# Root on VectorE, category rows by products, and more rows by address in a recommender kernel

## The chip, the core and the metric

The kernel runs on one core of a Trainium2 chip. The metric is device time in microseconds of one execution. Engines are named as in the profile: PE (TensorE), DVE (VectorE), ACT (ScalarE), POOL (GpSimd) and SP (SyncE). SP, ACT and POOL also issue DMAs; in the profile their issuing shows as SPq, ACTq and POOL.

## The reference

There are B = 16384 candidates, each with a user, an item, a category and a history of L = 200 items. Embeddings have 64 numbers.

```python
u = u_emb[user]; it = i_emb[item]; c = c_emb[cate]; h = i_emb[hist]     # h: (200, B, 64)
itb = jnp.broadcast_to(it[None], h.shape)
feat = jnp.concatenate([h, itb, h - itb, h * itb], axis=-1)
a = dice(feat @ au_W1 + au_b1, au_alpha, axis=1)    # mean and variance over B, per layer
w = a @ au_W2 + au_b2
cur = jnp.sum(w * h, axis=0)
z = jnp.concatenate([u, it, c, cur], axis=-1)
z = dice(z @ W1 + b1, alpha1, axis=0)
z = dice(z @ W2 + b2, alpha2, axis=0)
return z @ W3 + b3
```

dice(x) is x * (p + alpha * (1 - p)) with p = sigmoid((x - mean) / sqrt(var + 1e-8)). The item and user tables have 100,000 rows of 256 bytes, the category table has 1,000. All numbers are 32-bit floats. The work is dominated by 200 x 16384 rows of the item table.

## The kernel before

One history position l is a layer. A layer is cut into ND = 8 steps, and a step k = 8 l + c handles TD = 16 tiles of 128 rows (2048 candidates). A `rows` buffer holds the 16 tiles of a step, and there are 5 of these buffers.

Rows reach a buffer in two ways. Most tiles come by a gather: POOL issues one indirect DMA (L123) for 128 rows, with the row numbers from the tile `idx`. The last tile of some steps comes row by row: for the steps c in SIDES = (1, 3, 4, 5, 6, 7), SP and ACT load row addresses into registers (L293, up to 20 at a time) and issue one DMA of 256 bytes per row (L301) into one of 3 `side` buffers; ACT waits for all 128 rows on a semaphore (`await_rows`, L309) and copies the tile into its place in `rows` (`place`, L352). Step c = 5 does so only where l % 3 == 0 (SOMETIMES, EACH); otherwise its last tile is gathered with row numbers from `sidx`. So a layer with l % 3 == 0 has six tiles by address, and 122 gathers; the others have five, and 123 gathers. The rows by address of a layer are spread over its 8 steps, half of each step's on SP, half on ACT: 48 or 40 rows per step and queue.

The order is written out by hand; every engine runs its queue in that order. In step k: the gathers of step k; on ACT the hidden layer of step k - 2 (`hidden`, L339); at the end of a layer the statistics and the normalization (`moments`, `scale_and_shift`, L170 to L172, with the square root on ACT, which needs a table load before it and one after it, for the sigmoid); on ACT the sigmoid of step k - 9 (`gate`, L328); the wait and copy of the row tile of step k - 1; the row DMAs of step k; on DVE the transposes of step k - 1 (`turn`, L156), which also free the `rows` buffer for POOL; on PE and DVE the products of step k - 1; on DVE the statistics (L344), then `weights` (L331) and `weigh` (L335, L336) of step k - 9.

SP carries, besides its rows, the loads for the next layer: `idx` (L136) in step 0, `sidx` (L142) where needed, and the addresses (L145) in step 2.

In the prologue the items of all candidates are gathered (128 gathers) and transposed into `itT`, and the weights are loaded. The loop body covers 45 layers and runs 4 times, and 20 layers follow. In the tail, users and categories are gathered (256 gathers), a user step and a category step by turns, and the head is computed: the first layer with its statistics as the tiles come, then the rest.

Of the kernel before, what the change touches and what calls it, by code (L numbers as in the profile page):

```python
# [27 lines left out]
EACH = 3  # L28
LOAD = 20
ROW = 4 * D  # L30
# [4 lines left out]
def din_kernel(  # L35
# [76 lines left out]
    ids = [make(f"ids{i}", P, NT, dt=I32) for i in range(3)]  # L112
# [17 lines left out]
    def load_ids(t, v):  # L130
        nc.sync.dma_start(t[:, :NC], columns(v))
        for s in range(NS):
            nc.sync.dma_start(t[:, NC + s : NC + s + 1], col(v[(NC + s) * P : (NC + s + 1) * P]))

# [9 lines left out]
    def load_addresses(i, l):  # L144
        nc.sync.dma_start(addr[i], r_hist[ds(l, 1), NC * P :])  # L145
# [21 lines left out]
    def scale_and_shift(mean, var, rstd, shift):  # L167
        n = mean.shape[0]
        std = small.tile([P, 1], F32, tag="std", name="std")
        nc.scalar.activation(std[:n], var, AF.Sqrt, bias=eps[:n])  # L170
        nc.vector.reciprocal(rstd, std[:n])
        nc.vector.scalar_tensor_tensor(shift, mean, -1.0, rstd, ALU.mult, ALU.mult)  # L172

    eps = make("eps", P, 1)
# [14 lines left out]
    def attention_weights():  # L189
        nc.vector.memset(eps, EPS)  # L190
# [45 lines left out]
    def head_weights():  # L236
# [3 lines left out]
        for e in range(2):  # L240
            for g in range(2):
                r, d = quarter(e, g), ts(e, S)
                nc.sync.dma_start(w1a[r, :, ts(g, ZA)], w1[d, :, :ZA])
                nc.sync.dma_start(w1b[r, :, ts(g, ZB)], w1[d, :, ZA:])
        for g in range(2):
            nc.sync.dma_start(w2a[ts(g, ZA), g * ZA : g * ZA + Z2], W2[:ZA])
# [20 lines left out]
    flat = i_emb.rearrange("v d -> (v d)").bitcast(U8)  # L267

# [4 lines left out]
    def tiles_by_address(l):  # L273

        round_, i = divmod(l, EACH)
        first = round_ * (EACH * (NS - 1) + 1) + i * (NS - 1) + (i > 0)
        return first, [j for j, c in enumerate(SIDES) if has_side(l * ND + c)]

    def rows_by_address(k):
        l, s = divmod(k, ND)  # L280
        first, tiles = tiles_by_address(l)
        n = len(tiles) * P // ND // 2
        loads = -(-n // LOAD)
        for i, (engine, issue) in enumerate(
            ((mybir.EngineType.SP, nc.sync), (mybir.EngineType.Activation, nc.scalar))
        ):
            r0, end = (2 * s + i) * n, (2 * s + i + 1) * n
            while r0 < end:
                many = min(end - r0, -(-n // loads))
                at0 = tiles[r0 // P] * P + r0 % P  # L290
                while tiles[(r0 + many - 1) // P] * P + (r0 + many - 1) % P != at0 + many - 1:
                    many -= 1
                _, at = nc.values_load_multi_w_load_instructions(  # L293
                    addr[l % 3][:, at0 : at0 + many],
                    engines=(engine,), min_val=0, max_val=ROW * (V - 1),
                    skip_runtime_bounds_check_because="the DMA checks the address against the table",
                )
                for r, a in enumerate(at, r0):
# [9 lines left out]

    def await_rows(m):  # L309
        if m in keys:  # L310
            fence = nc.scalar.wait_ge(landed[m % 3], 16 * P)
            tc.declare_fence(fence.ins, group=keys.pop(m))
            nc.scalar.sem_clear(landed[m % 3])

    def has_side(k):
        l, c = divmod(k, ND)
        return c in SIDES and (c != SOMETIMES or l % EACH == 0)
# [28 lines left out]
    def place(k):  # L346
        if has_side(k):
            l, c = divmod(k, ND)
            first, tiles = tiles_by_address(l)
            m = first + tiles.index(SIDES.index(c))  # L350
            await_rows(m)
            nc.scalar.copy(rows[k % ROWS][:, TD - 1], side[m % 3])  # L352
# [30 lines left out]
    def step(k, last=None):  # L383
# [12 lines left out]
        if has(k - LAG):  # L396
            gate(k - LAG)
        if has(k - 1):
            place(k - 1)
        if has(k):  # L400
            rows_by_address(k)
        if has(k - 1):
# [5 lines left out]
        if has(k - LAG):  # L408
# [3 lines left out]
    def steps(l0, n, end):  # L412
        for k in range(n * ND):
            l, c = divmod(k, ND)
            if c == 0 and l + 1 < end:
                load_hist_ids((l + 1) % IDX, l0 + l + 1)
                if (l + 1) % EACH:
                    load_side_ids((l + 1) % IDX, l0 + l + 1)
            if c == 2 and l + 1 < end:
                load_addresses((l + 1) % 3, l0 + l + 1)  # L420
            if c == 4 and l + 1 < end:
                scale_addresses((l + 1) % 3)
            step(k)

    with tc.manual_schedule():
        load_ids(ids[0], r_item)
        load_hist_ids(0, 0)
        load_addresses(0, 0)
        load_ids(ids[1], r_cate)
        load_ids(ids[2], r_user)  # L430
        nc.gpsimd.iota(lanes, pattern=[[1, P]], base=P, channel_multiplier=-1)
        attention_weights()
        for t in (*hT, *xs, *side, hm):
            nc.vector.memset(t, 0.0)
        for t in curT:
# [7 lines left out]
        scale_addresses(0)  # L443
        layer(px, [(blk_m, hm)])

        for c in range(ND + 1):
            if c < ND:
                for n in range(TD):
                    j = column(c, n)
                    gather(rows[c % ROWS], ids[0][:, j : j + 1], n, i_emb)  # L450
            if c:
                transpose(itT[c - 1], rows[(c - 1) % ROWS])
        nc.vector.memset(rows[-1 % ROWS], 0.0)
# [17 lines left out]
    def head_fetch(k, j):  # L471
        c, u = divmod(j, 2)
        for n in range(TD):
            i = column(c, n)
            gather(rows[k % ROWS], ids[1 + u][:, i : i + 1], n, (c_emb, u_emb)[u])

    def head_layer(j):
        c, u = divmod(j, 2)
        if u == 0:
            pairs = ((2, ucT[j % 4]), (1, itT[c]), (3, curT[c]))  # L480
        else:
            pairs = ((0, ucT[j % 4]),)
# [118 lines left out]
```

## Time and profile before

| what | value |
|---|---|
| median of 10 runs | 51,004.96 us (50,974.05 to 51,075.69) |
| profiled execution: its time, its span | 50,960.83 us, 50,959.1 us |
| busy: PE, DVE, ACT, POOL | 41%, 30%, 9%, 46% of the span |
| row DMAs issued by SP, by ACT | 68,288 each |
| gathers on POOL | 24,533 of history, 128 of items, 128 of users, 128 of categories |
| mean granted TensorE clock | 0.694 |

Busy shares are of work in the engines; register instructions, semaphores and the issuing of DMAs by SP and ACT do not count as busy. In the lines of groups, the columns are: line, engine, operation, output and inputs, count, then busy time in all and nanoseconds of one, then idle time before them with what ended it. In a timeline, they are start, duration, engine, line, operation, tile and count, and in square brackets the idle time before.

### The profile page before, as it was taken

The page shows a single profiled execution, that of the slowest core. Times are in us where ns is not written, and L with a number is a line of the kernel's source. Part 1 is how long each engine was busy: PE and PEld are TensorE (multiplying, and loading weights), DVE is VectorE, ACT ScalarE, POOL GpSimd, SP SyncE. Part 2 cuts the span into 40 slices and gives each one's busy share as a digit, 9 for nine tenths or more (in the row PEclk, how much of TensorE's full clock was granted, in tenths as well). Part 3 has the DMA queues.
Part 4 walks back from the last instruction along what each step waited for, and adds up shares of the span by engine and source line. Part 5 has one row for each costly group of instructions (what it writes and reads, how often), then busy time and mean ns, then how long its engine had stood idle before and what let it go on. Part 6 is the DMA issues. An engine that isn't in the chain of part 4 may idle for free. (4 is left out here: it accounts for less than half of the span.)

```text
span 50959.1 us, 423966 instructions
## 1 busy us (share of the span) xinstructions
PE 20882.2 (41%) x38856; PEld 8541.7 (17%) x38856; DVE 15096.3 (30%) x18955; ACT 4416.1 (9%) x4941; POOL 23571.8 (46%) x24922
## 2 busy tenths in 40 slices
PE   3444444443444444444444444434444444444444
PEld 1111111111111111111111111111111111111111
DVE  2322232232222222222222222222223222222223
ACT  0000000000000000000000000000000000000001
POOL 5444444444444444444444444444444444444444
PEclk6666667676676666666676666666676666666667
DMA  1000100000000000000010001000000000100000
GB/s 19 18 17 17 18 17 18 17 17 18 18 18 17 17 18 17 17 18 17 17 18 17 17 18 18 17 17 18 17 18 18 18 17 18 18 17 18 18 17 17
DMA packets 1130924, 894.71 MB, mean 18 GB/s; under 512 B 729024, under 2 KB 729024, under 8 KB 1127896
## 3 DMA queue, kind: packets, MB, share of 16 engines
q0 software_dynamic: 797344, 818.07, 9.1%
q1 hardware_dynamic: 193112, 31.56, 0.4%
q10 hardware_dynamic: 137440, 17.76, 0.2%
q14 instruction: 2722, 22.30, 0.1%
q8 instruction: 306, 5.01, 0.0%
HBM read 865.10 MB, written 0.13 MB: 17 GB/s over the span
## 5 line engine op out<-in xcount | busy, mean ns | idle before, releaser
L123 POOL DMA_INDIRECT rows<-in_L_rec_i_emb,idx x24400 | 23082.3, 946 | 26994.0 <-DVE hT L156 19317.1
L161 PE MATMUL ph<-hT,unit 128*128 128x512 f32 x6404 | 5968.8, 1087 | 28850.7 <-DVE hT L156 27817.0
L335 DVE SCALAR_TENSOR_TENSOR wb<-wb,au_bias,hT 128x1024 f32<-128x1024 f32 x1609 | 2080.0, 1293 | 20967.4 <-remote 16592.7
L156 DVE STREAM_TRANSPOSE hT<-rows 64x512 f32<-64x512 f32 x6404 | 4516.2, 705 | 9866.5 <-ACT rows L352 9715.8
L161 PEld LDWEIGHTS ph<-hT,unit 128*128 128x128 f32 x6404 | 1798.6, 311 | 31910.2 <-DVE hT L156 30520.0
L339 ACT ACTIVATE xs<-px,au_bias 128x1024 f32<-128x1024 f32 x1602 | 1785.0, 1114 | 45005.6 <-issue 40412.7
L161 PE MATMUL px<-hT,blk_h 128*128 128x512 f32 x6404 | 4070.6, 723 | 979.2 <-ACT xs L339 623.6
L161 PE MATMUL px<-itT,blk_i 128*128 128x512 f32 x6404 | 3466.5, 624 | 0.0
L161 PE MATMUL wb<-y,blk_p 128*128 128x512 f32 x6436 | 3296.2, 594 | 46.8 <-issue 26.4
L161 PE MATMUL wb<-xs,blk_x 128*128 128x512 f32 x6436 | 3295.8, 594 | 27.0 <-DVE curT L336 16.8
L161 PE MATMUL px<-hm,blk_m 128*128 128x512 f32 x6408 | 3013.0, 592 | 69.5 <-remote 69.5
L344 DVE BATCH_NORM_STATS2 st<-xs 128x6 f32<-128x512 f32 x3204 | 2061.3, 685 | 2896.4 <-ACT xs L339 2232.0
L360 DVE TENSOR_TENSOR hm<-ph,itT 128x1024 f32<-128x1024 f32 x1601 | 1956.9, 1222 | 1659.8 <-PE ph L161 1285.1
L161 PEld LDWEIGHTS px<-hT,blk_h 128*128 128x128 f32 x6404 | 1609.1, 254 | 3531.9 <-issue 2700.5
L336 DVE TENSOR_TENSOR curT<-wb,curT 128x1024 f32<-128x1024 f32 x1609 | 1970.2, 1225 | 54.8
L331 DVE TENSOR_TENSOR y<-pg,xs 128x1024 f32<-128x1024 f32 x1609 | 1954.9, 1215 | 21.6 <-issue 21.4
L328 ACT ACTIVATE pg<-xs,sh,rs 128x1024 f32<-128x1024 f32 x1609 | 1934.1, 1202 | 30.8 <-DVE y L331 16.4
L161 PEld LDWEIGHTS px<-itT,blk_i 128*128 128x128 f32 x6404 | 1404.7, 219 | 1987.5 <-issue 1987.5
L161 PEld LDWEIGHTS wb<-y,blk_p 128*128 128x128 f32 x6436 | 1225.2, 190 | 1594.1 <-issue 1568.4
L161 PEld LDWEIGHTS wb<-xs,blk_x 128*128 128x128 f32 x6436 | 1224.5, 190 | 1573.8 <-issue 1553.3
L161 PEld LDWEIGHTS px<-hm,blk_m 128*128 128x128 f32 x6408 | 1218.0, 190 | 1604.5 <-issue 1534.3
L352 ACT COPY rows<-side 128x64 f32<-128x64 f32 x1068 | 251.2, 235 | 591.2 <-DMA side<-in_L_rec_i_emb 495.7
(155 smaller groups left out, 2148.3 us busy)
## 6 DMA issues: line engine op xcount, KB each, us to landing
side<-in_L_rec_i_emb SPq DMA_DIRECT2D x68288, 0.2 KB
side<-in_L_rec_i_emb ACTq DMA_DIRECT2D x68288, 0.2 KB
rows<-in_L_rec_i_emb,idx POOLq DMA_INDIRECT x24400
idx<-in_r_hist SPq DMA_DIRECT2D x200, 61.0 KB
addrs<-in_r_hist SPq DMA_DIRECT2D x200, 3.0 KB
sidx<-in_r_hist SPq DMA_DIRECT2D x133, 0.5 KB
rows<-in_L_rec_i_emb,sidx POOLq DMA_INDIRECT x133
rows<-in_L_rec_i_emb,ids POOLq DMA_INDIRECT x128
```

The costliest lines, as they stand in the source:

```text
L123: nc.gpsimd.indirect_dma_start(out=dst[:, n, :], out_offset=None, in_=table, in_offset=bass.IndirectOffsetOnAxis(ap=ids, axis=0),)
L156: nc.vector.transpose(by_tile(dst[ts(e, D)], i), of[ts(i, D), :, ts(e, S)])
L161: nc.tensor.matmul(dst[:, ts(i, CH)], lhsT, rhs[:, ts(i, CH)], start=(first and j == 0), stop=(last and j == len(pairs) - 1), skip_group_c ...
L328: nc.scalar.activation(pg, xs[k % XR], AF.Sigmoid, bias=shifts[i], scale=rstds[i])
L331: nc.vector.tensor_mul(y, pg, xs[k % XR])
L335: nc.vector.scalar_tensor_tensor(wb, wb, au_bias2, hT[k % LAG], ALU.add, ALU.mult)
L336: nc.vector.tensor_add(curT[k % ND], wb, curT[k % ND])
L339: nc.scalar.activation(xs[k % XR], px, AF.Identity, bias=au_bias)
L344: nc.vector.bn_stats(stats[l % 3][:, 2 * c + i, :], xs[k % XR][:, ts(i, CH)])
L352: nc.scalar.copy(rows[k % ROWS][:, TD - 1], side[m % 3])
L360: nc.vector.tensor_mul(hm, ph, itT[k % ND])
```

## The change

1. The square root and its reciprocal move from ACT to DVE: a first guess from the bits of the number by a shift and an integer-like multiply-add, then three Newton steps of three operations.
2. The wait for a row tile, the clearing of its semaphore and the copy into `rows` move from ACT to DVE.
3. Step c = 5 has its tile by address where l % 3 is 0 or 1 (MOST = 2): two layers of three have six tiles by address. In a step, all of SP's row DMAs and the first load's worth of ACT's stand ahead of the gate, the rest of ACT's after it.
4. In the prologue, the last tile of six of the eight item steps comes by address, 0.56 of the rows on SP. Meanwhile the category rows are made by products: the category numbers are laid out in order in memory, spread over 125 partitions, compared with 8 columns of values (`pick_categories`), and PE multiplies the table with the ones and zeros. The result, transposed as it is needed, is stored in memory (`catT`). Several zeroings go from DVE to ACT as copies of zeros.
5. In the tail there are 8 steps in place of 16: users are gathered, 5 of their tiles by address; the categories are loaded from `catT`; two steps of `gate`, `weights` and `weigh` are done per step while any are left. The weight rows of the category features are laid out for the new order.

```diff
--- before.py
+++ after.py
@@ -26,7 +26,9 @@
 SIDES = (1, 3, 4, 5, 6, 7)
 SOMETIMES = 5
 EACH = 3
+MOST = 2
 LOAD = 20
+SPLIT = 0.5
 ROW = 4 * D
...
-    ids = [make(f"ids{i}", P, NT, dt=I32) for i in range(3)]
+    ids = [make(f"ids{i}", P, NC, dt=I32) for i in range(2)]
...
     def scale_and_shift(mean, var, rstd, shift):
         n = mean.shape[0]
-        std = small.tile([P, 1], F32, tag="std", name="std")
-        nc.scalar.activation(std[:n], var, AF.Sqrt, bias=eps[:n])
-        nc.vector.reciprocal(rstd, std[:n])
+
+        v = small.tile([P, 1], F32, tag="v", name="v")
+        h = small.tile([P, 1], F32, tag="h", name="h")
+        v, h = v[:n], h[:n]
+        nc.vector.tensor_scalar_add(v, var, EPS)
+        nc.vector.tensor_single_scalar(h.bitcast(I32), v.bitcast(I32), 1, ALU.logical_shift_right)
+        nc.vector.tensor_scalar(
+            rstd.bitcast(I32), h.bitcast(I32), -1.0, float(0x5F375A00), ALU.mult, ALU.add
+        )
+        for _ in range(3):
+            nc.vector.scalar_tensor_tensor(h, rstd, v, rstd, ALU.mult, ALU.mult)
+            nc.vector.tensor_scalar(h, h, -0.5, 1.5, ALU.mult, ALU.add)
+            nc.vector.tensor_mul(rstd, rstd, h)
         nc.vector.scalar_tensor_tensor(shift, mean, -1.0, rstd, ALU.mult, ALU.mult)
...
                 r, d = quarter(e, g), ts(e, S)
-                nc.sync.dma_start(w1a[r, :, ts(g, ZA)], w1[d, :, :ZA])
-                nc.sync.dma_start(w1b[r, :, ts(g, ZB)], w1[d, :, ZA:])
+                for f in (slice(0, 2), slice(3, 4)):
+                    nc.sync.dma_start(w1a[r, f, ts(g, ZA)], w1[d, f, :ZA])
+                    nc.sync.dma_start(w1b[r, f, ts(g, ZB)], w1[d, f, ZA:])
+            nc.sync.dma_start(w1a[ts(g, D), 2, ts(g, ZA)], w1[:, 2, :ZA])
+            nc.sync.dma_start(w1b[ts(g, D), 2, ts(g, ZB)], w1[:, 2, ZA:])
...
-    def rows_by_address(k):
-        l, s = divmod(k, ND)
-        first, tiles = tiles_by_address(l)
-        n = len(tiles) * P // ND // 2
...
+    def shares(n, s, split):
+
+        many = round(n * split)
+        runs = []
+        for r0, end in ((s * n, s * n + many), (s * n + many, (s + 1) * n)):
+            loads = -(-(end - r0) // LOAD)
+            at = [r0 + (end - r0) * i // loads for i in range(loads + 1)]
+            runs.append(list(zip(at, at[1:])))
+        return runs
...
-                many = min(end - r0, -(-n // loads))
-                at0 = tiles[r0 // P] * P + r0 % P
-                while tiles[(r0 + many - 1) // P] * P + (r0 + many - 1) % P != at0 + many - 1:
+                many = end - r0
+                while place_of(r0 + many - 1) != place_of(r0) + many - 1:
...
+    def ask_hist(k, queue, some):
+        l, s = divmod(k, ND)
+        first, tiles = tiles_by_address(l)
+        runs = shares(len(tiles) * P // ND, s, SPLIT)[queue]
+        ask(queue, runs[some], first, tiles, addr[l % 3], i_emb)
+
+    def ask_all(s, split, first, n, at, table):
+        for queue, runs in enumerate(shares(NS * P // ND, s, split)):
+            runs = [(r0, min(end, n * P)) for r0, end in runs if r0 < n * P]
+            ask(queue, runs, first, range(n), at, table)
+
     def await_rows(m):
         if m in keys:
-            fence = nc.scalar.wait_ge(landed[m % 3], 16 * P)
+            fence = nc.vector.wait_ge(landed[m % 3], 16 * P)
             tc.declare_fence(fence.ins, group=keys.pop(m))
-            nc.scalar.sem_clear(landed[m % 3])
+            nc.vector.sem_clear(landed[m % 3])
-        return c in SIDES and (c != SOMETIMES or l % EACH == 0)
+        return c in SIDES and (c != SOMETIMES or l % EACH < MOST)
...
-            m = first + tiles.index(SIDES.index(c))
-            await_rows(m)
-            nc.scalar.copy(rows[k % ROWS][:, TD - 1], side[m % 3])
+            place_tile(k, first + tiles.index(SIDES.index(c)))
+
+    def place_tile(k, m):
+        await_rows(m)
+        nc.vector.tensor_copy(rows[k % ROWS][:, TD - 1], side[m % 3])
+
+    def fetch_all(k, c, ids, table):
+        for n in range(TD - (c in SIDES)):
+            j = column(c, n)
+            gather(rows[k % ROWS], ids[:, j : j + 1], n, table)
...
-        if has(k - LAG):
+        if has(k):
+            ask_hist(k, 0, slice(None))
+            ask_hist(k, 1, slice(0, 1))
+        if k - LAG not in weighed:
             gate(k - LAG)
+        if has(k):
+            ask_hist(k, 1, slice(1, None))
         if has(k - 1):
             place(k - 1)
-        if has(k):
-            rows_by_address(k)
-        if has(k - 1):
...
-        if has(k - LAG):
+        if k - LAG not in weighed:
             weights(k - LAG)
             weigh(k - LAG)
...
-                if (l + 1) % EACH:
+                if (l + 1) % EACH >= MOST:
                     load_side_ids((l + 1) % IDX, l0 + l + 1)
-            if c == 2 and l + 1 < end:
-                load_addresses((l + 1) % 3, l0 + l + 1)
-            if c == 4 and l + 1 < end:
+            if c == 2 and (l + 1 < end or then is not None):
+                load_addresses((l + 1) % 3, r_hist[ds(l0 + l + 1, 1)] if l + 1 < end else then)
+            if c == 4 and (l + 1 < end or then is not None):
                 scale_addresses((l + 1) % 3)
...
+    cs = [dram.tile([P, TD], I32, name=f"cs{c}") for c in range(ND)]
+    catT = [dram.tile([P, CD], F32, name=f"catT{c}") for c in range(ND)]
...
+    def spread_categories(q):
+        c, i = divmod(q, 2)
+        half = cs[c][ts(i, D)].rearrange("p n -> (p n)")
+        nc.scalar.dma_start(spread[q % SPREAD], half.partition_broadcast(PB))
+
+    def pick_categories(q):
+        for b in range(NB):
+            ones = xs[(q * NB + b) % XR][:PB]
+            nc.vector.tensor_scalar(
+                ones, spread[q % SPREAD], values[:PB, b : b + 1], None, ALU.is_equal
+            )
+            for g in range(2):
+                nc.tensor.matmul(
+                    bank[q % 8][ts(g, D)], table[:, b], ones[:, ts(g, CH)],
+                    start=b == 0, stop=b == NB - 1, skip_group_check=True,
+                )
+        nc.scalar.copy(
+            stages[q % 4].rearrange("p (n t) -> p n t", t=S),
+            bank[q % 8].rearrange("p (t n) -> p n t", n=TD),
+        )
+
+    def store_categories(q):
+        c, i = divmod(q, 2)
+        nc.scalar.dma_start(catT[c][:, ts(i, CH)], stages[q % 4])
...
-        load_ids(ids[0], r_item)
+        nc.sync.dma_start(ids[0], columns(r_item))
+        load_addresses(2, r_item.rearrange("(o b) -> o b", o=1))
+        order_categories()
         load_hist_ids(0, 0)
-        load_addresses(0, 0)
-        load_ids(ids[1], r_cate)
-        load_ids(ids[2], r_user)
+        load_addresses(0, r_hist[0:1])
+        nc.sync.dma_start(ids[1], columns(r_user))
...
+        for q in range(SPREAD - 1):
+            spread_categories(q)
...
+        scale_addresses(2)
+        nc.vector.memset(hm, 0.0)
+        for t in (*hT[SPREAD:], *curT[1:]):
+            nc.scalar.copy(t, hm)
+
+        for c in range(ND + 1):
+            if c < ND:
+                fetch_all(c, c, ids[0], i_emb)
+                ask_all(c, 0.56, -NS, NS, addr[2], i_emb)
+                for q in (2 * c, 2 * c + 1):
+                    pick_categories(q)
+                    if q + SPREAD - 1 < HALVES:
+                        spread_categories(q + SPREAD - 1)
+                    if q:
+                        store_categories(q - 1)
+            if c == 0:
+                attention_weights()
+                scale_addresses(0)
+            if c:
+                if c - 1 in SIDES:
+                    place_tile(c - 1, SIDES.index(c - 1) - NS)
+                transpose(itT[c - 1], rows[(c - 1) % ROWS])
+        store_categories(HALVES - 1)
+        layer(px, [(blk_m, hm)])
+        for t in xs:
+            nc.scalar.copy(t, hm)
+        for t in (*hT[:SPREAD], *side, curT[0], rows[-1 % ROWS]):
...
-    def head_fetch(k, j):
-        c, u = divmod(j, 2)
-        for n in range(TD):
-            i = column(c, n)
-            gather(rows[k % ROWS], ids[1 + u][:, i : i + 1], n, (c_emb, u_emb)[u])
...
+    user, category = ucT[:2], ucT[2:]
+
+    def head_layer(c, pairs, first):
+        layer(px, [(w1a[:, f], t) for f, t in pairs], first=first, last=not first)
+        layer(ph[:S], [(w1b[:, f], t) for f, t in pairs], first=first, last=not first)
...
+        steps(BODY, L - BODY, L - BODY, r_user.rearrange("(o b) -> o b", o=1))
+        U = addr[(L - BODY) % 3]
+        j = column(SIDES[-1], TD - 1)
+        nc.sync.dma_start(sidx[0], col(r_user[j * P : (j + 1) * P]))
+        first = -(-tiles_by_address(L - BODY)[0] // 3) * 3
+
+        weighed = set(range(-LAG, K - LAG))
+        for j in range(ND + 2):
+            if j < ND:
+                fetch_all(K + j, j, ids[1], u_emb)
+                if j == SIDES[-1]:
+                    gather(rows[(K + j) % ROWS], sidx[0], TD - 1, u_emb)
+                nc.sync.dma_start(category[j % 2], catT[j])
+            step(K + j, K - 1, weighed)
+            weighed.add(K + j - LAG)
             if j >= 2:
-                head_layer(j - 2)
+                k = max(weighed) + 1
+                if k < K:
+                    gate(k)
+                    weights(k)
+                    weigh(k)
+                    weighed.add(k)
+            if j < ND:
+                ask_all(j, SPLIT, first, NS - 1, U, u_emb)
+            if 1 <= j <= ND:
+                c = j - 1
+                head_layer(c, ((2, category[c % 2]), (1, itT[c]), (3, curT[c])), True)
+                if c in SIDES[:-1]:
+                    place_tile(K + c, first + SIDES.index(c))
+                transpose(user[c % 2], rows[(K + c) % ROWS])
+                head_layer(c, ((0, user[c % 2]),), False)
+                head_units(c)
```

## The prediction

> **What bounds the kernel now.** The run is 200 history layers of 8 steps between a prologue and a tail. I read the groups first, for the engine that is busiest, and it is none: POOL leads with 46%.
>
> ```profile
> L123 POOL DMA_INDIRECT rows<-in_L_rec_i_emb,idx x24400 | 23082.3, 946 | 26994.0 <-DVE hT L156 19317.1
> L352 ACT COPY rows<-side 128x64 f32<-128x64 f32 x1068 | 251.2, 235 | 591.2 <-DMA side<-in_L_rec_i_emb 495.7
> ```
>
> POOL issues a gather each 1.25 us (0.95 and 0.30 of gap), 15 or 16 to a step, then waits some 12 us for the transposes that free a row buffer. So POOL is early, not late. The page counts no DMA issue as busy, so I read what SP waits for, longest first.
>
> ```profile
> SPq L562 <- DVE res L553: 403.0, 2, 388.8
> SPq L293 <- remote: 76.3, 1, 76.3
> SPq L457 <- ACTq L311: 9.4, 4, 3.5
> ...
> SPq L301 <- ACT xs L339: 2.7, 11, 0.3
> ```
>
> The first is the tail, the second the prologue. In 50,434 us of row issue (112.8 to 50,546.5) SP waits for almost nothing: it is always issuing. Its timeline over two layers:
>
> ```profile
> 20359.44 0.36 SPq L136 DMA_DIRECT2D idx<-in_r_hist  x1
> 20361.40 59.53 SPq L301 DMA_DIRECT2D side<-in_L_rec_i_emb  x80
> ...
> 20423.12 177.57 SPq L301 DMA_DIRECT2D side<-in_L_rec_i_emb  x240
> 20601.16 0.36 SPq L136 DMA_DIRECT2D idx<-in_r_hist  x1
> 20601.73 0.36 SPq L142 DMA_DIRECT2D sidx<-in_r_hist  x1
> 20603.46 64.02 SPq L301 DMA_DIRECT2D side<-in_L_rec_i_emb  x96
> ...
> 20669.69 196.40 SPq L301 DMA_DIRECT2D side<-in_L_rec_i_emb  x288
> 20866.55 0.36 SPq L136 DMA_DIRECT2D idx<-in_r_hist  x1
> ```
>
> The idx load opens each layer on SP, so its starts are SP's clock. A five-tile layer (320 rows on SP) lasts 241.7 us, a six-tile layer (384 rows) 265.4. By all 200 starts the medians are 267.7 (l%3 = 0, six tiles), 242.6 (l%3 = 1) and 241.9 (l%3 = 2). **SP sets the time, and the number of row tiles sets SP's.**
>
> Within a step SP has two paces.
>
> ```profile
> 20095.71 11.30 SPq L301 DMA_DIRECT2D side<-in_L_rec_i_emb  x7
> 20108.40 6.68 SPq L301 DMA_DIRECT2D side<-in_L_rec_i_emb  x18
> 200.79 67.90 SPq L301 DMA_DIRECT2D side<-in_L_rec_i_emb  x24
> ```
>
> The second line lies where POOL rests: 18 rows with one address load of 1.23, hence 0.318 us a row. In the first, a burst of gathers is under way (POOL issues from 20,087.15 to 20,105.62): 1.6 us a row. The third lies in the long run of gathers of the prologue, 2.8 us a row. So each gather holds SP up. Adding up SP's start-to-start times over twelve layers, some 126 us a layer are over the free pace, with five tiles as with six, and a layer has 122 or 123 gathers: about 1.03 us of SP per gather.
>
> A rule bears on this. The Trainium skill, DMA: Bandwidth & Descriptors, SWDGE vs HWDGE vs iDMA, says that DMAs from SP and ACT do not pass through the descriptor ring that GpSimd writes and calls them immune to its interference. Read as "SP keeps its pace beside gathers", a six-tile step would cost SP 48 rows x 0.318 + 3 loads x 1.3 = 19.2 us and the row tiles would be free. The two paces above speak against that reading, and the sum goes by them.
>
> ACT is nearly as full, but it does wait:
>
> ```profile
> 20389.40 1.28 ACT L170 ACT_TABLE_LOAD   x1
> 20392.97 0.29 ACT L170 ACTIVATE std<-var,eps 128x1 f32<-128x1 f32 x1 [2.29 <-DVE var L380]
> 20393.29 1.28 ACT L328 ACT_TABLE_LOAD   x1
> ```
>
> **The change, part by part.** Base: the profiled execution, span 50,959.1, time 50,960.8; the median, 51,005, is 44 above it.
>
> *Root on VectorE, fence and copy on VectorE, part of the rows ahead of the gate.* ACT loses per layer 2 x 1.283 of table loads, 0.29, the 2.29 wait, 5.33 copies x 0.235 and 495.7/200 of landing waits: 8.9 us. DVE gains 12 tiny operations for the reciprocal (0.15 to 0.22 each by its neighbours' rows), less one: 2 us a layer, and a copy of about 0.15. DVE now holds the wait for the rows, and the transposes, statistics and products are queued behind it; but the transposes already waited for ACT's copy of the same rows (9,716 us in 1,063 waits), so nothing new is late. The gate on ACT (L328) now stands behind 16 or 20 rows, 6 us free or some 25 in a burst, and the product y on DVE (L331) waits for it; ACT no longer waits for rows and can do them early, and DVE then idles 13 us before wb anyway (20,968 us in 1,609), so I take 0 here too. ACT's 8.9 us fall on an engine that waits for SP's rows: I take 0. Bounds: +400 if DVE's 2 us all showed (200 x 2). Below nothing: ACT's rows go at 0.307 us free, SP's at 0.318; if a freer ACT left SP that pace, 68,288 x 0.011 = -750.
>
> *Six tiles in two layers of three.* l = 1, 4, ... 199: 67 layers get 64 more rows on SP, 64 more on ACT and one gather less. SP's price is read from the layer that has it: 267.7 - 242.6 = 25.1, x 67 = +1,682. From parts: 64 x 0.318 + 8 loads x 1.3 - 1.03 = 29.8, +1,997. Lowest, the rows alone less a gather: 19.3, +1,293. I take 25.1, a measured whole layer. The extra sidx load goes in 67 layers (start to start 0.57): -38. Loop: **+1,644**.
>
> *Prologue.* SP's start before: layer 0's rows begin at 112.8, but the next idx load comes at 490.96, so 223 us over a plain layer (490.96 - 267.7). In it lie some 35 us of small loads and 203 gathers (128 of items, 75 of history prefetched into the five buffers), hence 188/203 = 0.93 a gather, in line with 1.03. After: SP issues 0.56 of 768 item rows, 430 x 0.318 = 137, with 24 address loads x 1.3 = 31, and about 85 small loads x 0.46 = 39: 207 us; 122 + 75 gathers x 0.93 = 183. Together 390, so **+167**. Does anything outlast it? Categories: 256 calls of the matmul, two records each as in the rows of L161, 512 x 0.43 to 0.594 = 220 to 304 us on PE; 128 compares of 125x1024 on DVE at 0.80 (L525) to 1.22 (products) = 102 to 156; both lie under the eight item tiles (SP: 8 x (54 x 0.318 + 3 x 1.3 + 15 x 0.93) = 280). If that cover is gone, PE's upper value shows by 24. On ACT: 338 rows, 16 broadcasts of ids, 16 stores and some 35 copies of 0.6 to 1.1 come to less than SP's. Bounds +80 (SP free while POOL waits for buffers) to +250.
>
> *Tail.* Before, SP's last row is at 50,546 and the head's last unit ends at 50,872: 326 us for 192 remaining gathers (1.46 each, plus steps). After: 123 user gathers, some 64 issued ahead by then, and 640 user rows, 320 on SP in 7 steps: 320 x 0.318 + 21 x 1.3 + 59 x 1.03 = 190, then two steps of the head of about 20 (the spacing before): 230. SP's eight loads of the stored categories (0.4 each) are in that rounding. Bounds 175 to 266 (seven plain six-tile steps of 33.5 and the head's last 31), gain 60 to 150. I take **-90**. The 87 us after it stay, less some 5 for three roots.
>
> Sum: 50,961 + 1,644 + 167 - 90 = 52,682; with the 44 of the median **52,730**. Its own range: low 51,005 + 1,293 - 38 + 80 - 150 = 52,190; high 51,005 + 1,997 - 38 + 250 - 60 + 100 (a quarter of DVE's 400) = 53,250.
>
> **Rivals.**
> *Gathers set the step (faster).* The place is POOL's burst: if its length, not SP's rows, sets the step, 206 gathers fewer (67 of history, 6 of items, 133 of the head) pay 1.25 each, -258: **50,750**. For it: bursts slow every queue. Against it: POOL waits 12 us a step, SP never, and six-tile layers, with a gather fewer, last longer. It decides only if SP fits 64 more rows into a 242 us layer.
> *ACT sets the step (about the same).* ACT's 8.9 x 200 = -1,780 against +1,644 in the loop, +167 and -90: **50,950**. For it: ACT is full, and its relief is what the change does most. Against it: ACT waits 495.7 us for rows and SP's waits are nil. It decides if SP's issue time is itself stretched by ACT's.
> *The prologue drags (slower still).* In the run of gathers at 200 us SP gets one instruction in 1.4 us; if the 430 rows, the compares and the products crawl so while 92 gathers fill six tiles, 92 x 1.25 = 115 us are lost once, and with PE's upper end and a late start of the loop some 500: **53,250**.
>
> **Chances.** SP sets the time 0.74; gathers 0.10; ACT 0.07 (a third each for faster, same and slower); prologue 0.09. The range leaves out the first two rivals: 52,000 to 53,300. Its low end takes in the 750 of a freer SP (52,730 - 750), its high end the slow prologue. A difference under 0.2%, 100 us, can't be told from none. Faster 0.12, same 0.03, slower 0.85.
>
> **What would show it.** Right: SP's idx loads 265 to 269 us apart in layers l%3 = 0 and 1, about 242 in l%3 = 2; SP without waits; no table load for a root in the loop; POOL waiting longer than 12 us a step; the first idx load after layer 0 at about 650. Wrong: layers l%3 = 1 still near 242, SP waiting for side buffers, or six-tile layers under 260, which would mean that ACT had set the pace.

## The result and the profile after

| kernel | median | range, runs |
|---|---|---|
| before | 51,018.16 us | 50,958.61 to 51,114.60, 28 |
| after | 52,595.63 us | 52,543.81 to 52,692.89, 8 |

The ratio is 1.0309 (95% interval 1.0300 to 1.0318): the change makes the kernel slower by 3.1%. The span of the profiled execution is 52,527.5 us, 1,568.4 more than before.

The page's groups, the lines that answer to the two shown of before:

```profile
L125 POOL DMA_INDIRECT rows<-in_L_rec_i_emb,idx x24400 | 23080.5, 946 | 28650.4 <-DVE hT L153 20672.0
L382 DVE COPY rows<-side 128x64 f32<-128x64 f32 x1146 | 222.2, 194 | 10439.3 <-DMA side<-in_L_rec_i_emb 10417.8
```

The same number of these gathers at the same price (67 fewer come with the row numbers of `sidx`), and 1,656 us more of idle time on POOL before them: POOL has become earlier, not later. The copy of the row tile is on DVE now, and DVE waits 10,418 us for rows. What SP waits for:

```profile
SPq L684 <- DVE res L675: 117.3, 2, 104.5
SPq L310 <- DVE rows L382: 105.4, 156, 1.2
SPq L249 <- DVE w1b L243: 90.5, 1, 90.5
SPq L318 <- DVE rows L382: 40.8, 170, 0.6
```

The first is the end of the tail, the third the prologue. In 200 layers it waits some 150 us for side buffers (the second and fourth line), at most 1.2 at once. So SP is still always issuing, and its idx loads are still the clock of the layers. SP's timeline over a layer with l % 3 = 1, one with 2 and one with 0:

```profile
20094.58 0.36 SPq L133 DMA_DIRECT2D idx<-in_r_hist  x1
...
20096.90 63.84 SPq L318 DMA_DIRECT2D side<-in_L_rec_i_emb  x96
...
20361.19 0.36 SPq L133 DMA_DIRECT2D idx<-in_r_hist  x1
20363.16 57.61 SPq L318 DMA_DIRECT2D side<-in_L_rec_i_emb  x80
...
20606.98 0.36 SPq L133 DMA_DIRECT2D idx<-in_r_hist  x1
...
20872.83 0.36 SPq L133 DMA_DIRECT2D idx<-in_r_hist  x1
```

266.6 us with six tiles, 245.8 with five, 265.9 with six. Over all layers the medians are 264.8, 265.4 and 244.4 (l % 3 = 0, 1, 2), where before had 267.7, 242.6 and 241.9.

Cut at the first idx load after layer 0 and at the last layer's statistics, the two profiled executions give:

| stretch | before | after | difference |
|---|---|---|---|
| loop: idx load after layer 0 to last layer's aggregate | 50,074.8 | 51,522.1 | +1,447 |
| prologue: start to that idx load, less a six-tile layer | 223 | 438 | +215 |
| tail: to the first aggregate of the head | 307 | 215 | -92 |

They add up to 1,570.

**Chips of two kinds.** The experiments ran on four chips, and these do not agree on the kernel before: two took 51,276 and 51,418 us for it, as above (kind A: e5 to e8, e12), the other two 31,361 and 31,356 us (kind B: e1 to e4, e9 to e11). "Kind" is a name for what was seen: each of the four was used in one stretch of time only, so whether the difference stays with the chip is not shown. Every comparison below is with the kernel before on the same chip; a time of one kind is never set against one of the other, except to ask what differs.

### The profile page after: what moved, and what is told of

It reads as the page before. It is cut to its first block, busy times and chain, and to the rows that moved or that the text cites. A ratio compares the mean times of both kernels' runs of the same rounds, so it can differ in the third digit from the quotient of the medians.

```text
span 52527.5 us, 447483 instructions
## 1 busy us (share of the span) xinstructions
PE 21925.7 (42%) x39376; PEld 8790.7 (17%) x39376; DVE 15806.1 (30%) x22435; ACT 3816.1 (7%) x3299; POOL 23377.0 (45%) x24716
## 5 line engine op out<-in xcount | busy, mean ns | idle before, releaser
L158 PE MATMUL wb<-y,blk_p 128*128 128x512 f32 x6440 | 3822.9, 679 | 4538.1 <-DVE y L359 3595.0
L158 PE MATMUL wb<-xs,blk_x 128*128 128x512 f32 x6440 | 3592.5, 642 | 9.0 <-DVE curT L364 9.0
L382 DVE COPY rows<-side 128x64 f32<-128x64 f32 x1146 | 222.2, 194 | 10439.3 <-DMA side<-in_L_rec_i_emb 10417.8
L158 PEld LDWEIGHTS wb<-y,blk_p 128*128 128x128 f32 x6440 | 1345.7, 217 | 6421.8 <-DVE y L359 3823.5
```

The lines of the kernel that those rows point to most:

```text
L158: nc.tensor.matmul(dst[:, ts(i, CH)], lhsT, rhs[:, ts(i, CH)], start=(first and j == 0), stop=(last and j == len(pairs) - 1), skip_group_c ...
```

## Experiments

The theory tested is the prediction's: SP's issue of rows sets the time, a row tile costs some 25 us of SP in a layer, and each gather under way holds SP up by 1.03 us. The rivals are that POOL's gathers set it, and that ACT does.

### e1, e2, e3, e4: parts of the change (kind B)

e1 is the kernel before with the root, the wait for rows and the copy on VectorE, and nothing else:

```diff
-        nc.scalar.activation(std[:n], var, AF.Sqrt, bias=eps[:n])
-        nc.vector.reciprocal(rstd, std[:n])
+        # twelve operations on VectorE, as in the change
-            fence = nc.scalar.wait_ge(landed[m % 3], 16 * P)
+            fence = nc.vector.wait_ge(landed[m % 3], 16 * P)
-            nc.scalar.copy(rows[k % ROWS][:, TD - 1], side[m % 3])
+            nc.vector.tensor_copy(rows[k % ROWS][:, TD - 1], side[m % 3])
```

> The kernel before with only the root, the fence and the copy of the row tile moved from ScalarE to VectorE; row counts and order as before. Theory (SyncE's row issue sets the time): no change that counts, 50,800 to 51,150 us, layers on SyncE still 267.7, 242.6, 241.9 us within 3 us, SyncE still without waits. Rival (ScalarE sets the step): its 8.9 us a layer come off, about 49,240 us. Rival (gathers set the step): no change, but then VectorE must not wait longer for rows.

e2 is the kernel before with five tiles by address in every layer:

```diff
-        return c in SIDES and (c != SOMETIMES or l % EACH == 0)
+        return c in SIDES and (c != SOMETIMES or False)
```

> The kernel before with five tiles by address in every layer (step 5 never by address), 67 gathers more. Theory: 67 layers fall from 267.7 to about 242 us, 51,018 - 1,680 = 49,340 us (49,200 to 49,700), all layers on SyncE at 240 to 245 us. Rival (gathers set the step): 67 gathers more cost 1.25 to 2.0 us each, 51,100 to 51,150 us.

e3 is the changed kernel with five tiles in every layer, e4 with 45% of the rows on SP:

```diff
-MOST = 2
+MOST = 0          # e3
-SPLIT = 0.5
+SPLIT = 0.45      # e4
```

> The changed kernel with five tiles by address in every layer. Theory: its 134 six-tile layers fall from 265 to about 243 us, 52,596 - 134 x 22 = 49,650 us (49,300 to 50,000); beside the five-tile form of the kernel before it keeps the 215 us more in the prologue and the 92 less in the tail, so about 100 to 300 us above that. Rival (gathers): 134 gathers more, 52,760 us or above. Rival (ScalarE sets the step): relief and fewer rows add up, 47,800 us.

> The changed kernel with 0.45 of the rows of a step on SyncE in place of 0.5: 43 of 96 and 36 of 80, the rest (53 and 44) on ScalarE; row and gather counts are the same. Theory: SyncE loses 5 and 4 rows a step at 0.318 us, 12.7 and 10.2 us a layer, and the kernel falls by up to 134 x 12.7 + 66 x 10.2 = 2,370 us, if ScalarE has that room; ScalarE's longer share takes part of it, 50,400 to 51,800 us. Rival (gathers or VectorE set the step): no change, 52,500 to 52,700 us. Rival (ScalarE sets the step): slower, 53,800 to 55,000 us.

Measured, beside 31,361.44 us for the kernel before:

| run | time | ratio (95%) |
|---|---|---|
| e1 | 31,271.61 | 0.9949 (0.9928 to 0.9970) |
| e2 | 31,338.26 | 0.9992 (0.9971 to 1.0013) |
| e3 | 31,306.26 | 0.9969 (0.9947 to 0.9992) |
| e4 | 43,034.58 | 1.3688 (1.3654 to 1.3722) |

No theory expected times like these. The page of e1 says why: the same gathers, but almost no wait between them.

```profile
POOL 16%; issue 7%; ACTq 5%; PE 3%; DMA 2%; DVE 1%; ACT 0%; DVEq 0%; POOLq 0%; SPq 0%
...
L123 POOL DMA_INDIRECT rows<-in_L_rec_i_emb,idx x24400 | 23055.0, 945 | 7467.9 <-issue 7209.4
```

The first line is the chain that ended last, by engine: POOL leads it, SP is not in it. In the second, the 7,468 us of idle time are the gaps of 0.30 that POOL has between two gathers anyway; on kind A it was idle for 26,994. And SP's timeline in e1:

```profile
20077.99 0.36 SPq L136 DMA_DIRECT2D idx<-in_r_hist  x1
...
20080.53 30.81 SPq L310 DMA_DIRECT2D side<-in_L_rec_i_emb  x80
...
20113.56 104.96 SPq L310 DMA_DIRECT2D side<-in_L_rec_i_emb  x240
20218.99 0.36 SPq L136 DMA_DIRECT2D idx<-in_r_hist  x1
```

The same 80 rows that took 59.5 us in the prediction's trace take 30.8 here, with gathers under way all the time. On kind B hardly anything holds SP up (in e1, from one row of SP to the next, the median is 0.32 us), SP is ahead of POOL, and three layers of e1 (175.4 + 140.7 + 143.2 = 459.3 us) last as long as their 368 gathers at 1.249 us (459.6). So on kind B the rival "gathers set the step" holds, the sixth row tile of some layers is free or nearly so (e2, e3), and on kind A the prediction's theory could not be tested by these runs.

e4 has a cause of its own. Its shares of 43 and 53 rows in a step are loaded by 14, 15, 17 or 18 addresses. From start to start, an address load on ACT takes a median of 3.58 us, on SP 2.57; in e3, with loads of 20, it takes 1.50 and 1.51. ACT's timeline:

```profile
20016.22 1.21 ACT L356 ACTIVATE pg<-xs,sh,rs 128x1024 f32<-128x1024 f32 x1 [5.30 <-issue]
20019.84 13.31 ACTq L318 DMA_DIRECT2D side<-in_L_rec_i_emb  x30
```

For the 3.6 us from one line's start to the next's ACT issues no row: an address load of 3.48 runs beside the gate. ACT heads the chain of e4 (24%). From 5,000 to 25,000 us of the trace the loads take 7,171 us of ACT's queue and the rows 12,743, so that almost nothing is left of the 20,000. It is not the length of a load that makes it dear but the place where it begins. Set beside the kernel's list of addresses, the loads of e4 from 2,000 to 30,000 us fall into two sorts: those that begin at a multiple of four addresses took a median of 1.71 us on ACT and 1.63 on SP; those that begin elsewhere took 3.5 to 4.1 on ACT and 3.14 on SP. A load of 14 on SP took 1.43 in the first sort and 3.13 in the second. In e3, and in e10 below with its loads of 16 and 20, every load begins at a multiple of four.

### e5, e6, e7, e8: the theory where it applies (kind A)

> The changed kernel itself, as control. Two theories. Theory S: SP's issue of the rows by address sets the time (an address row costs SP 0.32 us free, each gather under way costs SP about 1.03 us more). Theory P: POOL's gathers set it, at 1.25 us each, because SP is not held up. The kernel before in the same call says which regime holds. If the kernel before takes about 51,000 us: S expects 52,600 (ratio 1.031), with idx loads on SP 265, 265 and 244 us apart; P expects 50,750. If the kernel before takes about 31,360 us: P expects (49.1 us for 67 six-tile layers with a gather less would be 67 x 1.25 = 84 us less, 133 gathers less in the tail 166, prologue with products about +50) 31,160, ratio 0.994; S, with 384 rows x 0.318 and 24 loads x 1.25 = 152 us for a six-tile layer on a free SP, also leaves POOL's 152.4 as the bound, but with SP so close that the ratio may be up to 1.02.

> The kernel before with the root, the wait for the rows and the copy of the row tile on VectorE, and nothing else of the change. If the kernel before takes about 51,000 us: theory S (SP sets the time) expects 50,900 to 51,100, no change, though ACT loses 8.9 us a layer; theory A (ACT sets the time, or its issue stretches SP's) expects up to 1,780 less, 49,200; the low end named in the prediction, a freer SP, is 50,250. If the kernel before takes about 31,360 us: 31,270 as before in such a run.

e7 leaves out every second gather of the history:

```diff
-        for n in range(TD - has_side(k)):
+        for n in range(0, TD - has_side(k), 2):
```

> The changed kernel without every second gather of the history (the rows of those tiles stay what they were in the buffer, so this part of the computation is left out): some 61 gathers a layer fewer; all rows by address, copies, products and sums stay. If the kernel before takes about 51,000 us: theory S with 1.03 us of SP per gather expects layers of 265 - 8 x 8 x 1.03 = about 200 us (l%3 = 0, 1) and 180 (l%3 = 2), and a time of 39,000 to 40,500; if gathers do not hold SP up and the rows cost what they cost whatever POOL does, 52,500. If the kernel before takes about 31,360 us: POOL needs only 61 x 1.25 = 76 us a layer, and SP's own free pace shows: 384 x 0.318 + 24 x 1.25 = 152 for six tiles, 127 for five, so 29,000 to 30,500 if SP or ACT is next, or less if they are faster than that.

```diff
-SIDES = (1, 3, 4, 5, 6, 7)
+SIDES = (5, 7)            # e8
-MOST = 2
+MOST = 3
```

> The changed kernel with two tiles by address in every layer (SIDES = (5, 7), MOST = 3), 126 gathers a layer, 128 rows on SP and 128 on ACT, one load of 16 addresses each per step. If the kernel before takes about 51,000 us: theory S expects a layer between 242.6 - 3 x 25.1 = 167 (the price of a tile, held over three tiles) and 128 x 0.318 + 8 x 1.25 + 126 x 1.03 = 181 us (from parts), so 34,300 to 37,000, much faster than both kernels; POOL's own 126 x 1.25 = 157 us a layer, 32,300 in all, is the floor. If the rows by address relieved the bound, as P says, it is slower by 3 x 1.25 x 200 = 750. If the kernel before takes about 31,360 us: P expects 126 x 1.249 = 157.4 a layer, 31,360 + 200 x 4.6 - the tail's gain of some 100 = 32,100 or a little more, slower by 2%; S expects no loss.

Measured, beside 51,275.92 us for the kernel before:

| run | time | ratio (95%) | layers, l % 3 = 0, 1, 2 |
|---|---|---|---|
| e5, the change | 52,926.42 | 1.0323 (1.0306 to 1.0340) | 267.6, 267.5, 246.0 |
| e6, relief alone | 50,723.57 | 0.9897 (0.9881 to 0.9914) | 266.7, 240.8, 240.7 |
| e7, half the gathers | 39,055.78 | 0.7616 (0.7604 to 0.7629) | 199.9, 200.1, 173.1 |
| e8, two tiles | 42,403.65 | 0.8270 (0.8256 to 0.8284) | 208.1, 207.7, 207.8 |

**e5** repeats the result. **e6** misses "no change": the relief of ACT is worth 552 us. It is no sign that ACT sets the time, which would have given three times as much; it lies inside the prediction's bound of 750 for a freer SP. Why a freer ACT makes SP faster was not tested. Against it the rest of the change costs 2,203 us. Cut as above, that is +2,126 in the loop, +189 in the prologue and -107 in the tail.

**e7** is the clearest. The gathers are 58 fewer in a six-tile layer and 59 fewer in a five-tile one; not one row by address is missing. SP's idx loads in e7:

```profile
20126.71 0.36 SPq L133 DMA_DIRECT2D idx<-in_r_hist  x1
...
20326.38 0.36 SPq L133 DMA_DIRECT2D idx<-in_r_hist  x1
...
20497.08 0.36 SPq L133 DMA_DIRECT2D idx<-in_r_hist  x1
```

That is 199.7 and 170.7 us. POOL's line shows the pauses:

```profile
L125 POOL DMA_INDIRECT rows<-in_L_rec_i_emb,idx x12800 | 12074.2, 943 | 26280.0 <-DVE hT L153 22395.6
```

POOL is idle for 26,280 us, SP still issues all the time, and its layers shrink by 67.6 and 72.9 us: 1.17 and 1.24 us for each gather left out. The gathers are on SP's bill without being on its queue.

**e8** beats both kernels and yet misses its range of 34,300 to 37,000: the three tiles taken away gave 38 us a layer (246.0 to 207.8), not 62 to 76. SP was no longer the bound, though not far from it: in 48 of the layers it runs out of scaled addresses and waits.

```profile
SPq L310 <- DVE addrs L145: 3144.1, 48, 68.5
```

What took its place was not tested; ACT's timeline shows a candidate:

```profile
4477.21 25.43 ACTq L318 DMA_DIRECT2D side<-in_L_rec_i_emb  x15
4502.69 1.21 ACT L356 ACTIVATE pg<-xs,sh,rs 128x1024 f32<-128x1024 f32 x1 [25.70 <-issue]
...
4511.85 5.28 ACTq L318 DMA_DIRECT2D side<-in_L_rec_i_emb  x16
```

In a run of gathers 15 rows take ACT 25.4 us, in POOL's pause 16 rows take 5.3. The gate stands behind the first, DVE's product behind the gate, the next transposes behind that, and the transposes free POOL's buffers.

### e9, e10, e11: fewer rows, another order (kind B)

e9 gathers all 128 tiles of a layer:

```diff
-SIDES = (1, 3, 4, 5, 6, 7)
-SOMETIMES = 5
+SIDES = (7,)
+SOMETIMES = 7
-MOST = 2
+MOST = 0
```

> The changed kernel with no history row by address: all 128 tiles of a layer are gathered (the items keep one tile by address, the users none). If the kernel before takes about 51,000 us: theory S says that SP's and ACT's issue of rows is the bound and stretches under the gathers; without it POOL's 128 x 1.25 = 160 us a layer is next, so 32,000 + some 250 for the item gathers and the prefetch + some 250 for the user gathers and the head = 32,500 to 33,000, over a third less than both kernels. The rival, that the gathers load the whole core and the tiles by address relieve it, expects 51,000 or more. If the kernel before takes about 31,360 us: the same 32,500 to 33,000 by both, 4% slower than before, since POOL then has 128 gathers in place of 123 in each layer.

```diff
+        if k - LAG not in weighed:       # e10: the gate ahead of the rows
+            gate(k - LAG)
         if has(k):
             ask_hist(k, 0, slice(None))
-            ask_hist(k, 1, slice(0, 1))
-        if k - LAG not in weighed:
-            gate(k - LAG)
-        if has(k):
-            ask_hist(k, 1, slice(1, None))
+            ask_hist(k, 1, slice(None))
```

> The changed kernel with the gate ahead of all row DMAs of its step on ACT, as it stood before. If the kernel before takes about 51,000 us: in the run of the relief alone a five-tile layer took 240.8 us and a six-tile one 266.7, in the changed kernel beside it 246.0 and 267.5, so some 66 x 5.2 + 134 x 0.9 = 460 us are not the tile's price. If the order of rows and gate is their cause, this kernel takes about 460 us less than the changed kernel in that run, a ratio to the kernel before of 1.023; five-tile layers 241, six-tile layers 267. If the order costs nothing, 1.032 and 246. If it helped, as an ACT that starts rows early would, 1.035 or more. If the kernel before takes about 31,360 us: POOL sets the time and the order changes it by under 0.5%.

> The changed kernel with four tiles by address in every layer (SIDES = (1, 3, 5, 7), MOST = 3). If the kernel before takes about 51,000 us: with SP as the bound a layer takes 246 less one tile's 21.5 to 25.9, that is 220 to 224.5, and the time is 44,600 to 45,700. With the mean price of the tiles between five and two, (246 - 208)/3 = 12.7, a layer takes 233 and the time is 47,400. If the rows by address relieve the bound, more than 52,900. If the kernel before takes about 31,360 us: POOL's 124 gathers give 124 x 1.249 = 154.9 a layer, 31,500 to 31,700.

Measured, beside 31,356.24 us for the kernel before: e9 32,450.57 (ratio 1.0349, 1.0332 to 1.0366), e10 33,027.69 (1.0532, 1.0515 to 1.0550), e11 31,487.21 (1.0045, 1.0030 to 1.0059). e9 and e11 fall where POOL's count puts them: layers of 159.8 us for 128 gathers (1.248 each) and 154.1 for 124 (1.243). e10 misses "under 0.5%": its layers take 174.8, 170.5 and 139.3 us on SP, together 484.6, where their 367 gathers at 1.249 need 458.4. (The sum of three counts here: on this kind SP's idx loads are uneven even where POOL sets the time, as in e1.) The chain that ended last in e10, by engine:

```profile
ACTq 18%; issue 5%; POOL 3%; PE 2%; DVE 2%; ACT 2%; DMA 1%; SPq 0%; DVEq 0%; POOLq 0%
```

So in e10, with the gate first and six tiles in two layers of three, ACT's queue is the bound. The changed kernel as it stands was not run on a chip of kind B, and e10 not on one of kind A: what the order of gate and rows is worth stays open on both.

### e12: no row by address (kind A)

> The kernel with no history row by address once more (128 gathers a layer), to see it beside a kernel before of about 51,000 us, where the rows by address were seen to be slow to issue. In that case: SP and ACT have almost nothing to issue that the gathers can hold up, POOL is the bound with 128 x 1.25 = 160 us a layer, and the time is 32,400 to 33,000, a ratio of 0.63 to 0.65; if the gathers held up ACT's two activations a step, DVE or PE in the same way (1.03 us for each gather under way and 16 gathers a step), a step would last 16 x 1.25 and some 6 to 16 more, 208 to 290 us a layer, 42,000 or more. If the kernel before takes about 31,360 us: 32,450 as measured, ratio 1.035.

42,128.51 us beside 51,418.49, a ratio of 0.8192 (0.8178 to 0.8205): the low end of the second expectation, not the first. SP and ACT have next to nothing to issue here, POOL could do a layer in 160 us, and a layer takes 207. The group of the first operation on DVE that waits for PE's sums says where the time is; of e9 (kind B) and of e12 (kind A), the same kernel:

```profile
L365 DVE SCALAR_TENSOR_TENSOR wb<-wb,au_bias,hT 128x1024 f32<-128x1024 f32 x1610 | 2080.9, 1292 | 10870.7 <-PE wb L158 10870.7
```

```profile
L365 DVE SCALAR_TENSOR_TENSOR wb<-wb,au_bias,hT 128x1024 f32<-128x1024 f32 x1610 | 2081.1, 1293 | 24147.2 <-remote 18550.4
```

On kind B the releaser is PE. On kind A most of the idle time ends on "remote": no work in the profile ended when this operation began. One case of it, by the tile `wb` (first and last start of each operation) and by POOL's timeline:

```profile
L158 PE MATMUL wb<-y,blk_p x4: 593/593/593, 10026.1 to 10028.3; 128*128 128x512 f32 x4
L365 DVE SCALAR_TENSOR_TENSOR wb<-wb,au_bias,hT x1: 1293/1293/1293, 10045.3 to 10045.3; 128x1024 f32<-128x1024 f32 x1
```

```profile
10039.17 0.95 POOL L125 DMA_INDIRECT rows<-in_L_rec_i_emb,idx  x1 [0.30 <-issue]
10050.91 0.95 POOL L125 DMA_INDIRECT rows<-in_L_rec_i_emb,idx  x1 [10.80 <-DVE hT L153]
```

PE's last product ends at 10,028.9. DVE, idle since 10,022, starts at 10,045.3: 16.4 us later, and 5.2 us after POOL's last gather has ended (10,040.1). Then DVE transposes, POOL's buffers come free, and POOL's next run begins. It is not DVE that is slow to see the signal: the trace also records when the semaphore that DVE waits for was raised, and in 532 of the 533 late steps counted below that was within 0.1 us of DVE's start. Whether PE's products ended late or their signal did cannot be told apart, since the profile models the ends of products.

The same run of gathers, which began at 10,000.4, also has a step that was on time:

```profile
10011.86 1.29 DVE L365 SCALAR_TENSOR_TENSOR wb<-wb,au_bias,hT 128x1024 f32<-128x1024 f32 x1 [6.94 <-PE wb L158]
...
10045.31 1.29 DVE L365 SCALAR_TENSOR_TENSOR wb<-wb,au_bias,hT 128x1024 f32<-128x1024 f32 x1 [23.34 <-remote]
```

From 2,000 to 30,000 us of the trace DVE started over 3 us late in 533 of 1,079 steps, and 526 of these starts lie in a pause of POOL. Most runs there are of 32 gathers, two steps long. Of the steps whose products ended 9 to 12 us into a run none of 530 was late; of those that ended 24 to 30 us into it all 524 were. In e9 it was 0.04 us late throughout, in none of 1,401 steps more than 3. In e7, kind A with runs of 8 gathers, 3 of 1,171 were. In the prediction's own trace, of the kernel before with runs of 15 and 16, where SP and ACT issue rows beside the gathers, products that end 9 to 12 us into a run are already late in 762 of 802 steps; the median lateness is 6.7 us, and 493 of the 816 late starts come while the run still goes on.

So on kind A a long run of gathers holds up more than SP's issue: what PE signals some way into the run reaches DVE and ACT late, in e12 mostly not before POOL pauses. By what path is not shown. With rows by address this lay hidden behind SP; without them the loop of POOL, DVE and the freed buffers takes 26 us a step (207/8) in place of POOL's 20. e8 takes as long, but must have another reason: only 64 of its 1,072 steps were over 3 us late.

## Why the prediction was right

Predicted 52,730, measured 52,596. The mechanism held, but that the total came so close is in part luck: a gain of 552 us and a loss of some 390, both put at nothing, largely cancel. Step by step:

- **SP sets the time.** Shown for kind A: SP has no wait that counts after the change, six-tile layers are where they were put (265 to 269 predicted, 264.8 and 265.4 measured), and POOL is earlier (12.9 us of wait for transposes a step, 12.1 before).
- **A tile costs 25.1 us in a layer.** Right in size in the order of the kernel before: 25.9 in e6. In the changed order six- and five-tile layers differ by less, 20.7 (21.5 in e5). The loop gave +1,447 where +1,644 was put, 197 less. Both ends of the term moved: layers with six tiles in both kernels are 2.9 us shorter than before (264.8 to 267.7), layers with five in both 2.5 longer (244.4 to 241.9). (The price from parts is 29.7, not 29.8, which changes little.)
- **ACT's relief is worth 0.** This step failed, and by more than the whole sum shows. e6 gives -552. The reason offered, that the relief falls on an engine that waits for SP anyway, forgot what the bound beside it said: if all of it lies in the loop, SP itself got faster by some 2.8 us a layer (552/200). The prediction came out well because the rest of the change took it back: in the loop of e5 over that of e6, 67 tiles at 25.9 are 1,735 of 2,126. The other 390 lie mostly in the five-tile layers (246.0 against 240.7, some 350), which have the same tiles and gathers in both. The new order of rows and gate is one candidate; that was not settled.
- **Prologue +167.** +215 measured, inside its bounds. The failed step is the one that found nothing to outlast SP's item rows. They were done at 343; then SP stood still for 90.5 us before the head's weights. That wait alone is more than the miss of 48, so SP's issue itself, put at 390, was some 40 too dear (438 less 90.5 is 347.5). The first idx load after layer 0 came at 703 where about 650 was named. DVE's timeline of that moment:

```profile
388.77 0.26 DVE L554 MEMSET side<- 128x64 f32 x3
429.80 0.91 DVE L554 MEMSET curT<- 128x1024 f32 x1 [40.77 <-remote]
```

PE's last product of the categories ends at 388.1, and the zeroing that waits for it begins at 429.8. POOL's run of prefetch gathers goes from 324.9 to 422.1. It looks like the late signal of e12 (the semaphore was raised at 429.5); the rival of the dragging prologue named the run, but as slow issue and not as a signal held back.
- **Tail -90.** -92 measured, -107 in e5 against e6. The sum fits; no run tests its terms.
- **VectorE's additions cost 0.** Nothing contradicts it, and nothing separates it: it lies within e6's gain.
- **1.03 us of SP per gather.** 1.17 to 1.24 for those that e7 left out, and its time (39,056) is in the expected range. It is no fixed price: at 1.17 for each of the 64 gathers that stay in a six-tile layer of e7, 199.9 - 75 = 125 us would be left for 384 rows and 24 loads that take 153 at the free pace of the prediction's rows (0.318 and 1.3). So the gathers of a shorter run cost SP less. The trace of the kernel before shows how: from 2,000 to 30,000 us the median from one row of SP to the next is 0.32 us in the first 3 us of a run of gathers, 1.0 from 3 to 6, 1.4 from 6 to 9, 2.1 from 9 to 15 and 2.8 after that. The 1.03 is the mean over runs of 15 and 16.

Of the rivals, "gathers set the step" is false on kind A and true on kind B, where SP issues 80 rows beside the gathers in 30.8 us. The prediction weighed a rule of the Trainium skill (DMA: Bandwidth & Descriptors, SWDGE vs HWDGE vs iDMA): DMAs from SP and ACT do not use the rings that GpSimd writes, and so are immune when VectorE locks GpSimd out of them. That is not a sentence on how fast SP issues. Read as "SP keeps its pace beside gathers", kind B agrees (30.8 us for 80 rows), and kind A does not (59.5): the row decided for the chip on which it was taken, and only for chips like it. "ACT sets the step" is false on kind A by e6; on kind B ACT is the bound in e10.

## What to carry to other kernels

Find the engine that never waits, even where the page counts it as idle, and read the price of a change from the stage that already has it: one layer with six tiles gave the price of one tile more. It did not hold for three tiles fewer (38 us in e8, not 75). Where a profile shows an operation that starts long after the work it needs has ended, and its wait ends on "remote", look at what else paused just then. And a balance between two ways to fetch rows, tuned where one of them is held up, need not hold elsewhere: all-gathered rows are 18% faster on one kind of chip and 3.5% slower on the other. The root, the wait and the copy on VectorE alone are a small gain on kind A (0.9897); on kind B (0.9949) they lie within the spread of the kernel before.

## What was not expected of the hardware

- Two kinds of chip: the kernel before takes 51,018 to 51,418 us on the one (the prediction's runs, e5 to e8, e12) and 31,356 to 31,361 on the other (e1 to e4, e9 to e11), with gathers of some 0.945 us at 1.25 us spacing on both. Why they differ is not shown.
- On the first kind a run of gathers slows SP the more the longer it lasts: from row to row 0.32 us in its first 3 us, 2.8 after 15 us (the kernel before). In runs of 32 gathers a signal from PE reached DVE 16 us late in every second step (e12).
- Loading 14 to 18 addresses into registers took 1.6 to 1.7 us where the load began at a multiple of four addresses, and 3.1 to 4.1 elsewhere (medians, e4).
